# Moving vector work of stages 2 to 4 and of the keys onto GpSimd and ScalarE in an eight-block cross-attention network

## The chip, the cores and the metric

The kernel runs on one core of a Trainium2 chip, as one program of 39,917 instructions. A core has five engines with an instruction queue each: TensorE (PE in the profile, with its weight loads as PEld) multiplies matrices and transposes by multiplying with an identity; VectorE (DVE), ScalarE (ACT) and GpSimd (POOL) work on tiles of 128 partitions; SyncE (SP) starts most DMAs. Engines run their own queues in order and wait for each other through semaphores. The metric is device microseconds (us) from start to end. Before the change the median of 3 runs was 3399.83 us (3399.31 to 3401.43).

## The reference

The input x is four sequences of 512 tokens with 512 features (2,048 tokens). Eight blocks are applied one after the other, alternating cross-attention and feed-forward, each on a layer-normalised x, gated and added:

```python
x = x + jnp.tanh(g_xattn[1]) * _L1_xattn_ref(_layernorm(x), ctx_1024, ...)
x = x + jnp.tanh(g_ffn[1])   * _L1_ffn_ref(_layernorm(x), weight, w_scale, bias)
x = x + jnp.tanh(g_xattn[2]) * _L2_xattn_ref(ctx_1024, _layernorm(x), ...)
```

These three are the kernel's stages 2, 3 and 4, which the change touches. Stage 2 makes attention weights from the context (four sequences of 512 rows with 256 features) and mixes x's features with them:

```python
energy = jnp.einsum('bnd,bmd->bnm', query, key)
attention = jax.nn.softmax(energy, axis=-1)
x_m = jnp.einsum('bln,bmn->blm', teacher_logits, attention)
```

Stage 3 is a quantised linear layer, with one scale per token:

```python
absmax = jnp.max(jnp.abs(x), axis=-1, keepdims=True)
scale = jnp.maximum(absmax, eps) / 127.0
q = jnp.clip(jnp.round(x / scale), -128, 127).astype(jnp.int8)
acc = jnp.einsum('bsk,nk->bsn', q, weight, preferred_element_type=jnp.int32)
out = acc.astype(jnp.float32) * in_scale * w_scale[:, 0] + bias
return out.astype(jnp.float16)
```

Stage 4 is a state-space layer: its scan result y depends on the context alone, and only its last step, `y = y * silu(z)` with z the normalised x, needs the x of that moment. Stage 5 is a mixture of experts that begins with normalisation and a router product. Stage 6, much later, is an attention whose keys and values come from the context alone (`ctx @ Wkv`, 32 heads of 16), with a rotation of the keys by position:

```python
out = jnp.stack([x1 * cos - x2 * sin, x1 * sin + x2 * cos], axis=-1)
```

## The kernel before

All of x stays in SBUF as 16 tiles of 128 tokens by 512 features. A batch b is one sequence, that is four tiles t. The stages run one after the other, each as a loop over four batches (`NB`) with an inner loop over four tiles (`TB`). The class `Net` has small helpers, which appear in the profile under their own lines: `ln` (L193, statistics at L175 and L176, a square root on ACT at L179, the normalising DVE instruction at L200), `lnT` (normalise, transpose on PE at L218, copy out of PSUM through `evict`), `transposed` (four PE transposes at L228 and one copy), `chain` (a chain of matrix products into one PSUM bank, L238) and `residual` (L729, one DVE instruction that does x += r * gate). `evict(i, ...)` copies a PSUM bank to SBUF, on ACT (L161) when i is odd and on DVE (L163) when it is even.

Stage 2 (`s2`, L813), per batch: queries and keys from the context (L238, bias on DVE), then for each tile m the energies (PE, L834), the negated row maximum (DVE, L839), the exponential with its sum (ACT, L841), the reciprocal (DVE, L842), the division by the sum (DVE, L843) and the transposition of the weights into aT; then `lnT` of x, and for each tile a product of four matrix multiplications and the residual.

Stage 3 (`s3`, L856), per batch: normalise four tiles, absolute maxima (DVE, L869), scales. Then for each tile, scale and round to an integer by adding MAGIC = 1.5 * 2^23 (DVE, L877), shift back and clip below (DVE, L880), clip above and convert to bf16 (DVE, L882), four transposes (PE, L886), a copy qT (alternately DVE and ACT), the product po (PE, L238), the dequantisation r (DVE, L892), bias and conversion to float16 (DVE, L896), the residual (DVE, L729).

Stage 4 (`s4`, L1082), per batch: the stored y by DMA, normalise x into g, SiLU over all four tiles in one ACT instruction (L1093, with a load of the function table), four products g * y (DVE, L1095), then for each tile four transposes (PE, L1099) and the residual. Its normalisation needs only its own batch of x, so a batch of stage 4 can begin while stage 3 is at work on the next.

Beside these three stages, a generator `keys()` computes stage 6's keys and values. There are 16 of them, one for each tile of context. Each step makes the product `pkv` (16 matrix multiplications, two banks: keys and values), rotates the keys with six DVE instructions that read PSUM (`rope`, L1426 to L1429, into one of two padded tiles `ropes`), copies the values on ACT (L1514) and stores them, and then transposes and stores the keys of the step before (`keyT`, PE L1447, ACT L1531). The function `aside(n)` draws n such steps into the stage at the place where it is called: two per batch in `s2`, one in `s3`, one in `s4`.

The order on each engine is not written by hand. The framework's scheduler goes over the whole program when it is built, with the place in the program as priority, and fixes the order of every engine's queue; `aside` lifts its instructions a little:

```python
def aside(n):
    with tc.high_priority(offset=-400):
        for _ in range(n):
            next(keys, None)
```

Tiles come from pools of rotating buffers: the pool `tp` gives 512-wide working tiles (tag "t", ten of them), `ps1` single PSUM banks (four), `ps2` double banks (two, shared by pkv and the transposed keys), `wp` 2,048-wide tiles (eight). A new tile waits until the last reader of the buffer's former content is done.

Of the kernel before, what the change touches and what calls it, by code (L numbers as in the profile page):

```python
# [9 lines left out]
F32 = mybir.dt.float32  # L10
# [5 lines left out]
AF = mybir.ActivationFunctionType  # L16
ALU = mybir.AluOpType
AX = mybir.AxisListType

P = 128  # L20
# [4 lines left out]
TB = S // P  # L25
# [23 lines left out]
class Net:  # L49
# [153 lines left out]
            outs.append(xl)  # L203
        return outs

    def lnT(self, name, b, rows=None, room=None):

        nc = self.nc
        xl = self.ln(name, self.x[b * TB : (b + 1) * TB])
        if rows is not None:  # L210
            for i in range(TB):
                t = b * TB + i
                nc.sync.dma_start(rows[t * P : (t + 1) * P, :], xl[i])
        xT = (room or self.u)(f"xT_{name}").rearrange("p (c n) -> p c n", c=DC)
        for c in range(DC):
            pt = self.mm(f"pt_{name}_{c}")
            for i in range(TB):
                nc.tensor.transpose(  # L218
                    pt[:, i * P : (i + 1) * P], xl[i][:, c * P : (c + 1) * P], self.ident
                )  # L220
            self.evict(c, xT[:, c, :], pt)
        return xT

    def transposed(self, name, src, dst, i=0, tied=False):
# [585 lines left out]
    def s2(self, aside):  # L810
# [5 lines left out]
        for b in range(NB):  # L816
# [15 lines left out]
            for m in range(TB):  # L832
                pe = self.mm(f"s2_pe_{b}_{m}")
                nc.tensor.matmul(  # L834
                    pe, lhsT=qk[0][:, m * P : (m + 1) * P], rhs=qk[1], start=True, stop=True
                )
                nmx = self.s(f"s2_nmx_{b}_{m}", 1, "s2_nmx")
                sm = self.s(f"s2_sm_{b}_{m}", 1, "s2_sm")
                nc.vector.tensor_reduce(nmx, pe, axis=AX.X, op=ALU.max, negate=True)  # L839
                at = self.t(f"s2_at_{b}_{m}")  # L840
                nc.scalar.activation(at, pe, AF.Exp, bias=nmx, accum_out=sm)  # L841
                nc.vector.reciprocal(sm, sm)  # L842
                nc.vector.tensor_scalar(at, at, sm, None, op0=ALU.mult)  # L843
                self.transposed(f"s2_{b}_{m}", at, aT[:, :, m * P : (m + 1) * P], m)
            xT = self.lnT(f"s2_{b}", b, room=self.w)
            aside(2)
            for t in range(TB):
                po = self.mm(f"s2_po_{b}_{t}")
# [6 lines left out]
    def s3(self, aside):  # L855
# [5 lines left out]
        nc.vector.tensor_copy(w, w8.bitcast(I8))  # L861
        wsc = self.bcast("s3_wsc", a["s3_wsc"])
        bias = self.bcast("s3_bias", a["s3_bias"])
        for b in range(NB):
            xl = self.ln(f"s3_{b}", self.x[b * TB : (b + 1) * TB])
            aside(1)
# [8 lines left out]
            for t in range(TB):  # L875
                q = xl[t]
                nc.vector.tensor_scalar(  # L877
                    q, q, rsc[:, t : t + 1], MAGIC, op0=ALU.mult, op1=ALU.add
                )
                nc.vector.tensor_scalar(q, q, -MAGIC, -128.0, op0=ALU.add, op1=ALU.max)  # L880
                qb = self.tp.tile([P, 512], BF16, tag="t", name=f"s3_q_{b}_{t}")
                nc.vector.tensor_scalar(qb, q, 127.0, None, op0=ALU.min)  # L882
                pt = self.ps1.tile([P, 512], BF16, tag="mm", name=f"s3_pt_{b}_{t}")
                for c in range(DC):
                    cs = slice(c * P, (c + 1) * P)
                    nc.tensor.transpose(pt[:, cs], qb[:, cs], self.ident16)  # L886
                qT = self.tp.tile([P, 512], BF16, tag="t", name=f"s3_qT_{b}_{t}")
                self.evict(t, qT, pt)
                po = self.mm(f"s3_po_{b}_{t}")
                self.chain(po, [(qT[:, c * P : (c + 1) * P], w[:, c, :]) for c in range(DC)])  # L890
                r = self.t(f"s3_r_{b}_{t}")
                nc.vector.scalar_tensor_tensor(  # L892
                    r, po, isc[:, t : t + 1], wsc, op0=ALU.mult, op1=ALU.mult
                )
                h = self.tp.tile([P, 512], F16, tag="t", name=f"s3_h_{b}_{t}")
                nc.vector.tensor_tensor(h, r, bias, op=ALU.add)  # L896
                self.residual(b * TB + t, h, self.gf[:, 1:2])


# [183 lines left out]
    def s4(self, aside):  # L1083
        nc = self.nc
        EC = DC
        for b in range(NB):
# [5 lines left out]
            self.ln(f"s4_{b}", self.x[b * TB : (b + 1) * TB], out=g)  # L1092
            nc.scalar.activation(g4, g4, AF.Silu)  # L1093
            for e in range(EC):
                nc.vector.tensor_tensor(g[:, e, :], g[:, e, :], y[:, e, :], op=ALU.mult)  # L1095
            for t in range(TB):
                pt = self.mm(f"s4_pt_{b}_{t}")
                for e in range(EC):
# [316 lines left out]
        self.wt5 = wt  # L1415


    def rope(self, name, ps, t, out):

        nc = self.nc  # L1420
        H = 32
        x = ps.rearrange("p (m h k) -> p m h k", m=2, h=H)
        cos, sin = (v[:, t, :].unsqueeze(1).to_broadcast([P, H, 8]) for v in self.trig)
        for i in range(2):
            tmp = self.t(f"rt_{name}_{i}")[:, 0 : H * 8].rearrange("p (h k) -> p h k", h=H)
            dst = out[:, :, 8 * i : 8 * i + 8]  # L1426
            nc.vector.tensor_tensor(tmp, x[:, 1, :, :], (sin, cos)[i], op=ALU.mult)
            nc.vector.tensor_tensor(dst, x[:, 0, :, :], (cos, sin)[i], op=ALU.mult)
            nc.vector.tensor_tensor(dst, dst, tmp, op=(ALU.subtract, ALU.add)[i])  # L1429

    def padded(self, name, n, fill):

# [18 lines left out]
    def keys(self):  # L1451
# [52 lines left out]
        for b in range(NB):  # L1504
            cx = self.context("s6", b)
            for k in range(TB):
                ks = slice(k * P, (k + 1) * P)
                pkv = self.sc(f"s6_pkv_{b}_{k}")
                for i in range(2):
                    half = slice(512 * i, 512 * (i + 1))  # L1510
                    self.chain(pkv[:, i, :], [(cx[:, c, ks], wkv[:, c, half]) for c in range(CC)])
                self.rope(f"k_{b}_{k}", pkv[:, 0, :], b * TB + k, ropes[k % 2])
                v = vs[k % 2]
                nc.scalar.copy(  # L1514
                    v[:, 0 : H * 17].rearrange("p (h d) -> p h d", d=17)[:, :, 0:16],
# [459 lines left out]
```

## Time and profile before

| What | Value |
|---|---|
| Median of 3 runs | 3399.83 us |
| Profiled execution (its span) | 3401.39 us (3399.4 us) |
| PE busy | 2880.1 us, 85% of the span |
| DVE busy | 1975.8 us, 58% |
| ACT busy | 1197.1 us, 35% |
| POOL busy | 627.9 us, 18% |
| Mean granted TensorE clock | 0.920 of full speed |
| Stage 2 | about 1527 to 1678 us |
| Stage 3, and stage 4 beside it | about 1678 to 1811 us |
| End of stage 4, start of stage 5 | about 1811 to 1853 us |

The span is the time from the first instruction to the last in one execution; the time of that execution lies 2.0 us above it. The busy shares are means over the whole program. The three stretches at the bottom are 326 us, about a tenth of it, so the shares say little about them; each has to be read by itself. A line of the tables by group reads: source line, engine, operation, output<-input by the program's names, shape and count, then busy us and mean ns of one, then the time that the engine was idle just ahead of these instructions and what ended it. In the tables of waits, "A <- B" says that A waited for B. The granted clock is the share of full speed at which the chip's throttle let PE run.

### The profile page before, as it was taken

How to read it: one execution, taken by the hardware profiler on the slowest of the kernel's cores; microseconds unless marked ns; L12 is line 12 of the kernel's file. 1: busy time of each engine (PE TensorE's matmuls, PEld its weight loads, DVE VectorE, ACT ScalarE, POOL GpSimd, SP SyncE). 2: the span in 40 equal slices, each digit the busy share in tenths (PEclk: the TensorE clock that was granted, in tenths of full speed). 3: DMA queues.
4: the chain of work that ended last, by engine and by line, in shares of the span. 5: the costliest groups of instructions: out<-in, count | busy, mean ns of one | idle time of the engine just before them, and what ended most of it. 6: DMA issues, size and time to landing. Idle time of an engine off the chain costs nothing.

```text
span 3399.4 us, 39917 instructions
## 1 busy us (share of the span) xinstructions
PE 2880.1 (85%) x14620; PEld 1432.3 (42%) x14624; DVE 1975.8 (58%) x3148; ACT 1197.1 (35%) x1927; POOL 627.9 (18%) x509
## 2 busy tenths in 40 slices
PE   4889898968998989998836699968898988889995
PEld 2333333223444444444414588842233332244673
DVE  5555555558797989975687311137666666634103
ACT  1243333355544454433222111112544444520231
POOL 0000000005564655760000122210000000000341
PEclk9799999988998999999967699987999999989997
DMA  3000000047675876861212599971000000022698
GB/s 125 7 1 7 1 1 9 1 160 227 195 230 177 241 223 202 250 188 57 84 63 85 177 324 325 325 250 50 13 27 13 27 1 1 1 75 78 245 385 314
DMA packets 266338, 438.56 MB, mean 129 GB/s; under 512 B 32368, under 2 KB 114544, under 8 KB 264608
## 3 DMA queue, kind: packets, MB, share of 16 engines
q1 hardware_dynamic: 247776, 382.52, 35.3%
q0 software_dynamic: 13760, 45.10, 3.7%
q10 hardware_dynamic: 4608, 8.39, 0.7%
q8 instruction: 117, 1.92, 0.2%
q14 instruction: 77, 0.63, 0.1%
HBM read 370.79 MB, written 65.13 MB: 128 GB/s over the span
## 4 chain that ended last, share of the span: by engine, by line
PE 38%; DVE 9%; issue 3%; DMA 2%; POOL 2%; ACT 1%; SPq 0%; POOLq 0%; DVEq 0%; ACTq 0%
PE s_po L238 8%; PE s_pl L262 7%; PE pg_s L238 6%; PE s_av L262 4%; DVE s_top L1656 2%; PE s_ph L238 2%; PE s_pq L238 2%; PE s_ps L262 1%; PE s_pkv L238 1%; PE s_pr L238 1%; DVE x L729 1%; DMA s_y<-s_ys 1%; PE pt_s L218 1%; POOL s_ys L1321 1%; PE s_pb L238 1%
## 5 line engine op out<-in xcount | busy, mean ns | idle before, releaser
L1012 POOL TENSOR_TENSOR s_h<-s_h,s_C 128x512 f32<-128x512 f32 x256 | 447.2, 1747 | 295.7 <-DVE s_h L1011 249.7
L1656 DVE TENSOR_REDUCE s_top<-s_ps 128x1 f32<-128x512 f32 x512 | 330.1, 686 | 162.6 <-PE s_ps L262 158.4
L1766 ACT ACTIVATE pr_s<-s_pl 128x512 f32<-128x512 f32 x512 | 277.9, 595 | 344.2 <-PE s_ps L262 327.1
L1011 DVE TENSOR_TENSOR_SCAN s_h<-s_da,s_db 128x512 f32<-128x512 f32 x256 | 312.0, 1219 | 62.8 <-PE s_y L262 37.1
L262 PE MATMUL s_pl<-s_qT,s_kT 32*128 32x512 f32 x1024 | 291.4, 642 | 63.4 <-DVE s_top L1656 59.0
L262 PE MATMUL s_ps<-s_kT,s_qT 32*128 32x512 f32 x1024 | 306.6, 668 | 6.1 <-DVE s_top L1656 5.8
L1010 ACT ACTIVATE s_da<-s_rdl,s_A 128x512 f32<-128x512 f32 x256 | 184.3, 722 | 329.3 <-DVE s_h L1011 328.7
L238 PE MATMUL s_ph<-xT_s,s_wu 128*128 128x256 f32 x1024 | 250.4, 400 | 0.7 <-ACT xT_s L161 0.7
L771 PE MATMUL s_acc<-s_wd,s_hT 128*128 128x512 f32 x512 | 239.9, 612 | 6.8 <-ACT s_hT L802 6.8
L238 PEld LDWEIGHTS s_ph<-xT_s,s_wu 128*128 128x128 f32 x1024 | 199.9, 200 | 79.3 <-issue 48.4
L238 PEld LDWEIGHTS pg_s<-s_xbT,s_w 128*128 128x128 f32 (+1 forms) x1872 | 214.1, 183 | 19.8 <-issue 17.8
L599 DVE TENSOR_REDUCE s_nmx<-ps_s 128x2 f32<-128x992 f32 x128 | 151.4, 1184 | 116.7 <-PE ps_s L262 116.7
L238 PE MATMUL pg_s<-s_xbT,s_w 128*128 128x128 f32 (+1 forms) x1872 | 215.7, 275 | 1.4 <-ACT s_xbT L161 1.4
L262 PE MATMUL s_av<-pr_s,s_v 128*32 128x512 f32 (+1 forms) x1536 | 209.6, 617 | 0.8 <-ACT pr_s L1766 0.7
L1009 DVE TENSOR_TENSOR s_db<-s_B,s_rdu 128x512 f32<-128x512 f32 x256 | 202.7, 792 | 10.5 <-DMA s_B<-s_bc 2.7
L714 ACT ACTIVATE pr_s<-pl_s 128x1024 f32<-128x1024 f32 (+1 forms) x128 | 130.9, 1022 | 192.1 <-PE pl_s L262 161.7
L262 PE MATMUL s_y<-s_h,ident 64*64 64x512 f32 x1024 | 146.5, 635 | 47.1 <-issue 30.0
L1400 DVE TENSOR_TENSOR g_s<-g_s,pg_s 128x256 f32<-128x256 f32 x78 | 27.5, 353 | 263.9 <-ACT g_s L1399 263.9
L262 PEld LDWEIGHTS s_pl<-s_qT,s_kT 32*128 32x128 f32 x1024 | 80.0, 184 | 232.9 <-ACT pr_s L1766 197.7
L262 PE MATMUL pl_s<-s_qT,s_kT 32*128 32x512 f32 (+1 forms) x512 | 151.1, 667 | 26.1 <-ACT pr_s L714 23.0
L262 PE MATMUL ps_s<-s_kT,s_qT 32*128 32x496 f32 x512 | 156.1, 713 | 4.5 <-DVE s_nmx L599 4.1
L771 PEld LDWEIGHTS s_acc<-s_wd,s_hT 128*128 128x128 f32 x512 | 93.4, 192 | 151.9 <-issue 116.4
(376 smaller groups left out, 4269.7 us busy)
## 6 DMA issues: line engine op xcount, KB each, us to landing
s_B<-s_bc SPq DMA_DIRECT2D x256, 256.0 KB
s_C<-s_bc SPq DMA_DIRECT2D x256, 256.0 KB
s_w<-in_s_wg SPq DMA_DIRECT2D x39, 704.0 KB
s_w<-in_s_wu SPq DMA_DIRECT2D x39, 704.0 KB
s_w_rt<-in_s_ru SPq DMA_DIRECT2D x47, 512.0 KB
s_w_rt<-in_s_rd SPq DMA_DIRECT2D x47, 512.0 KB
s_w<-in_s_wd SPq DMA_DIRECT2D x39, 512.0 KB
s_y<-s_ys SPq DMA_DIRECT2D x32, 512.0 KB
```

Source lines behind the costliest of these rows:

```text
L218: nc.tensor.transpose(pt[:, i * P : (i + 1) * P], xl[i][:, c * P : (c + 1) * P], self.ident)
L238: ins = self.nc.tensor.matmul(out, lhsT=l, rhs=r, start=(i == 0), stop=(i == len(pairs) - 1)).ins
L262: ins = self.nc.tensor.matmul(out, lhsT=l, rhs=r, **flags).ins
L599: i = nc.vector.tensor_reduce(nmx[:, at : at + 2], ps[:, :, 0:M], axis=AX.X, op=ALU.max, negate=True,)
L714: nc.scalar.activation(prs[i][0:n], pl[0:n], AF.Exp)
L771: ins = nc.tensor.matmul(accs[i][t], lhsT=hT[:, j, t * P : (t + 1) * P], rhs=wd[f // 4][:, f % 4, :], start=(f == 0), stop=(f == FC - 1),).ins
L1009: nc.vector.tensor_tensor(db, br, du, op=ALU.mult)
L1010: nc.scalar.activation(da, dl, AF.Exp, scale=am[:, e, n : n + 1])
L1011: nc.vector.tensor_tensor_scan(h, da, db, 0.0, op0=ALU.mult, op1=ALU.add)
L1012: nc.gpsimd.tensor_tensor(h, h, cr, op=ALU.mult)
L1656: ins = nc.vector.tensor_reduce(dst[:, i], ps[i], axis=AX.X, op=ALU.max, negate=True).ins
L1766: exps.append(nc.scalar.activation(prs[i][:, j, :], pl[j], AF.Exp).ins)
```

## The change

Work is put on other engines in five places; what is computed stays the same, and so do tiles and loops.

- Stage 2: the division of the weights by their sum goes from DVE to ACT; all copies of transposed weights and of transposed x go to ACT instead of alternating.
- Stage 3: the clip becomes one DVE instruction on the values that still carry MAGIC; the shift back by MAGIC, with the conversion to bf16, becomes an ACT activation with a bias tile `less`; the copy qT is always on ACT; the bias is added on GpSimd; the conversion to float16 is a copy on ACT.
- Stage 4: the products g * y go from DVE to GpSimd.
- Keys: ACT copies the key half of pkv to an SBUF tile `kr` (two buffers), and the six rotation instructions run on GpSimd from there.

```diff
     def lnT(self, name, b, rows=None, room=None, turns=(0, 1)):
...
-            self.evict(c, xT[:, c, :], pt)
+            self.evict(turns[c % 2], xT[:, c, :], pt)
...
                 nc.vector.reciprocal(sm, sm)
-                nc.vector.tensor_scalar(at, at, sm, None, op0=ALU.mult)
-                self.transposed(f"s2_{b}_{m}", at, aT[:, :, m * P : (m + 1) * P], m)
-            xT = self.lnT(f"s2_{b}", b, room=self.w)
+                nc.scalar.mul(at, at, sm)
+                self.transposed(f"s2_{b}_{m}", at, aT[:, :, m * P : (m + 1) * P], 1)
+            xT = self.lnT(f"s2_{b}", b, room=self.w, turns=(1, 1))
...
         bias = self.bcast("s3_bias", a["s3_bias"])
+        less = self.s("s3_less", 1)
+        nc.gpsimd.memset(less, -MAGIC)
...
-                nc.vector.tensor_scalar(q, q, -MAGIC, -128.0, op0=ALU.add, op1=ALU.max)
+                nc.vector.tensor_scalar(
+                    q, q, MAGIC - 128.0, MAGIC + 127.0, op0=ALU.max, op1=ALU.min
+                )
                 qb = self.tp.tile([P, 512], BF16, tag="t", name=f"s3_q_{b}_{t}")
-                nc.vector.tensor_scalar(qb, q, 127.0, None, op0=ALU.min)
+                nc.scalar.activation(qb, q, AF.Identity, bias=less)
...
-                self.evict(t, qT, pt)
+                self.evict(1, qT, pt)
...
+                nc.gpsimd.tensor_tensor(r, r, bias, op=ALU.add)
                 h = self.tp.tile([P, 512], F16, tag="t", name=f"s3_h_{b}_{t}")
-                nc.vector.tensor_tensor(h, r, bias, op=ALU.add)
+                nc.scalar.copy(h, r)
                 self.residual(b * TB + t, h, self.gf[:, 1:2])
...
             for e in range(EC):
-                nc.vector.tensor_tensor(g[:, e, :], g[:, e, :], y[:, e, :], op=ALU.mult)
+                nc.gpsimd.tensor_tensor(g[:, e, :], g[:, e, :], y[:, e, :], op=ALU.mult)
...
-    def rope(self, name, ps, t, out):
-
-        nc = self.nc
+    def rope(self, name, ps, t, out, engine=None):
+
+        engine = engine or self.nc.vector
...
-            nc.vector.tensor_tensor(tmp, x[:, 1, :, :], (sin, cos)[i], op=ALU.mult)
-            nc.vector.tensor_tensor(dst, x[:, 0, :, :], (cos, sin)[i], op=ALU.mult)
-            nc.vector.tensor_tensor(dst, dst, tmp, op=(ALU.subtract, ALU.add)[i])
+            engine.tensor_tensor(tmp, x[:, 1, :, :], (sin, cos)[i], op=ALU.mult)
+            engine.tensor_tensor(dst, x[:, 0, :, :], (cos, sin)[i], op=ALU.mult)
+            engine.tensor_tensor(dst, dst, tmp, op=(ALU.subtract, ALU.add)[i])
...
-                self.rope(f"k_{b}_{k}", pkv[:, 0, :], b * TB + k, ropes[k % 2])
+                kr = self.kp.tile([P, 512], F32, tag="kr", name=f"s6_kr_{b}_{k}", bufs=2)
+                nc.scalar.copy(kr, pkv[:, 0, :])
+                self.rope(f"k_{b}_{k}", kr, b * TB + k, ropes[k % 2], nc.gpsimd)
```

## The prediction

> **What bounds the kernel now.** I read the view of the core first (mean granted clock 0.920), then the page's slices to find stages 2 to 4 (about 1527 to 1855 us), then the table of windows over that stretch, its groups of instructions, its waits and its chain of waits. The table has length, then busy time (and instructions) of PE, weight loads, DVE, ACT and POOL, then the granted clock:
>
> ```profile
> 1527.00:1678.00 151.00, 126.26 (x410) 63.88 (x410) 90.36 (x219) 46.98 (x79) 0.00 (x0) 0.98 0.22 71
> 1678.00:1811.00 133.00, 67.59 (x241) 32.36 (x244) 108.12 (x245) 28.34 (x33) 0.00 (x0) 0.71 0.19 61
> 1811.00:1853.00 42.00, 24.07 (x113) 16.45 (x112) 33.40 (x77) 10.65 (x14) 0.00 (x0) 0.77 0.14 49
> ```
>
> Stage 2 is PE's: 84% busy at almost full clock. In stage 3 DVE is busy 81% and PE half, at a reduced clock. POOL does nothing in any of them. The groups of 1678 to 1853 (busy us and mean ns, then idle before) and the waits of 1526 to 1856 say who waits for whom:
>
> ```profile
> L892 DVE SCALAR_TENSOR_TENSOR s_r<-s_po,s_isc,s_wsc 128x512 f32<-128x512 f32 x16 | 12.0, 751 | 22.5 <-PE s_po L238 22.5
> ...
> L896 DVE TENSOR_TENSOR s_h<-s_r,s_bias 128x512 f16<-128x512 f32 x16 | 11.0, 688 | 0.3
> ...
> L1095 DVE TENSOR_TENSOR s_g<-s_g,s_y 128x512 f32<-128x512 f32 x16 | 10.3, 683 | 0.2 <-ACT s_g L1093 0.2
> ```
>
> In the waits (waiter, releaser, total us, times, longest):
>
> ```profile
> PEld L886 <- DVE s_q L882: 57.5, 12, 17.8
> ```
>
> PE waits 57.5 us for the quantised tile; DVE waits 22.5 us for the product that PE then makes. So stage 3 is no queue of DVE work alone: within a batch it is a ring, and between batches a DVE stretch. The ring in the chain of waits (start, length, step), batch 1, tiles 2 to 3:
>
> ```profile
> 1734.69 0.76 DVE s_r L892
> ...
> 1735.48 0.69 DVE s_h L896
> ...
> 1737.06 0.59 ACT s_qT L161
> ...
> 1737.70 1.08 PE s_po L238 x4
> ...
> 1738.80 0.76 DVE s_r L892
> ```
>
> One turn is 4.1 to 4.5 us: L892, L896, L882 (420 ns in the groups, between s_h and s_qT), four transposes, the copy, the product. From L892's starts in the timeline the three turns take 13.10, 13.27, 16.99 and 16.99 us in batches 0 to 3 (60.35), and the stretches between batches 16.70, 20.71 and 16.72 (54.13). In batches 2 and 3 the product takes 1.89 instead of 1.04 us. In the tail PE's timeline shows keys standing behind stage 4's last batch, and the chain going through the rotation and a key's product (another follows at 1845.61):
>
> ```profile
> 1829.96 3.76 PE L1099 MATMUL s_pt<-ident,s_g 128*128 128x128 f32 x16 [11.56 <-DVE s_g L1095]
> ...
> 1838.92 4.70 PE L238 MATMUL s_pkv<-s_wkv,ctx_s 128*128 128x512 f32 x8 [0.38 <-ACT s_vs L1514]
> ```
>
> **Prices and the Trainium skill.** POOL's only like work is stage 4's scan (min/median/max ns, then two lines of its timeline):
>
> ```profile
> L1012 POOL TENSOR_TENSOR s_h<-s_h,s_C x256: 1264/1772/3506, 779.3 to 1510.7; 128x512 f32<-128x512 f32 x128
> ...
> 1493.23 0.70 DVE L1009 TENSOR_TENSOR s_db<-s_B,s_rdu 128x512 f32<-128x512 f32 x1
> 1493.28 1.77 POOL L1012 TENSOR_TENSOR s_h<-s_h,s_C 128x512 f32<-128x512 f32 x1 [2.48 <-DVE s_h L1011]
> ```
>
> "SBUF — State Buffer", Who interferes with whom, says that DVE and GpSimd exclude each other for a whole instruction when DVE has two SBUF inputs or a two-port mode. The trace agrees: POOL takes 1.26 us at best and 1.77 beside DVE's 0.70 product. "GPSIMD Engine Reference", 3.1, gives about 2.6 cycles an element at 1.2 GHz for two inputs. Half of a 512 row is then 0.55 us less than 1.264: I estimate 0.71 us for a 256-wide rotation step (no run shows one; bounds 0.6 and 1.3, the upper with contention). "ScalarE: Activation LUTs", What ACT_TABLE_LOAD costs, has 280 + 0.833 N ns for an ACTIVATE with a pointer operand, 707 at 512; the exponential here takes 687, so I take 0.7 for the new division and the last shift. Copies are 0.59 (s_qT) in the trace. "TensorE: Matmul & The Clock Gate", What's actually happening, says that an idle PE falls to half clock; the windows agree (1.00 at 1685 to 1705, 0.50 at 1745 to 1765).
>
> **The change, part by part.** The built programs' order shows where each instruction now stands; durations are of the profiled run.
>
> Removed from DVE in stages 3, 4 and the tail: L896 16 x 0.69, L882 16 x 0.42, eight s_qT copies x 0.42, L1095 16 x 0.68, and 51 rotation steps x 0.41: 11.0 + 6.7 + 3.4 + 10.3 + 21 = 52 us of busy time. The new clip replaces L880 at its 0.42. This would be the gain only if DVE's busy time were the length.
>
> Stage 2. The division goes from 0.49 on DVE to 0.7 on ACT: +0.2 on the path for the first tiles of a batch; for tile 3 it had queued behind normalisation, and saves some 0.3. All eight matmul records of a key's product now stand ahead of the next tile's transposes, where half (1.88) lay under the softmax: +0.5 to +1.7 in three batches, taken as 0.6. The xT copies, all on ACT at 0.59, keep up with PE, which uses one block per 0.43 and started after 1.75: nothing, or 1.2 lost without that cover. Sum +2 (-2 to +6). The rotation leaves DVE under PE's 13.7 us of products: nothing.
>
> Start of stage 3. PE goes from stage 2's last product into two keys' products and then s3's transposes, which no longer wait for the rotation's 14 steps on DVE: first L892 3.0 earlier. On POOL its bias stands behind one key's six steps: +1.4. Sum -1.6.
>
> The ring, the part that decides. DVE's order in the changed program is L892, then that tile's residual, which waits for ACT's copy of h, which waits for POOL's bias. On ACT the copy of h of tile t stands ahead of the shift of tile t+1. So a turn is L892 0.75, POOL 1.27, h 0.60, shift 0.70, to the copy 0.55 (transposes, as from L882's end to s_qT now), copy 0.58, product 1.04, and 0.2 of gaps: 5.7 us; 6.6 where the product takes 1.89. What was one DVE queue step of 0.69 plus 0.42 is now four steps on two engines. Batch 0: 3 x 5.7; batch 1: 5.7 + 2 x 6.6; batches 2 and 3: 6 x 6.6: 75.6. POOL also has four gate products (5.1 us) ahead of a bias in batches 2 and 3, started by ACT's SiLU, which itself stands ahead of h: +1.5 and +2.5. Sum 79.6 against 60.35: +19. This assumes that PE stays cold; if it doesn't, 5.7 x 12 + 4 = 72.4, +12.
>
> Between batches. DVE's front (four normalisations 0.46, four maxima 0.6, statistics, scale and clip) reaches the first clipped tile in 9.5 after L892, with the residual's wait in it; ropes and stage 4's normalisation no longer stand in it. POOL's rotation steps contend with it, +1. Then shift 0.7, transposes 0.55 to copy, the second half of a key's product 1.7 in between, product 1 to 1.9: 5. So 15.5 each, and 2.3 more where gate products stand ahead of the last bias of batch 2: 48.8 against 54.13: -5.3.
>
> Tail. From the end of the last L892 (1810.96) to the first router product (1854.65) are 43.7 us. Now: last bias 1.3, a key's four last steps to 4.2, its transposes to 6.3, stage 4's transposes with a key's product among them to 15.8 (K half 12.3), copy and rotation to 17.2, the next key's product to 21, its rotation to 25; table load and SiLU on ACT to 27; four gate products on POOL, behind all rotations, to 32.1; transposes, then four residuals on DVE ahead of the router's first copy: 36.4. Sum -7.3 (-12 to 0). What is late next there is POOL.
>
> Sum: +2 - 1.6 + 19 - 5.3 - 7.3 = +6.8 on a profiled execution of 3401.39 us (span 3399.4). That execution is 1.6 over the median of 3399.83, within the runs' own spread, so I add to the median: 3406.6, forecast 3407. Below 0.2% (6.8 us) I call it no change, as far as a measurement tells.
>
> **Rivals.** (a) Faster, 3390: PE keeps its clock and POOL's rotation hides. For: POOL is idle now, and DVE loses 52 us. Place: the ring, at the turn of 5.7 instead of 6.6 in all batches (-7), with no front contention (-3) and gate products never ahead of a bias (-6.3): -16 to -17. It decides once transposes and product see a clock above about 0.8. Against: PE idles over 60% of a turn. (b) A tie, 3400: the tail gives back 12 rather than 7 and stage 2 is free; 6.8 - 4.7 - 2 = 0. For: PE's 11.56 us wait goes. (c) GpSimd becomes the bound, 3424: steps at 1.3 us instead of 0.71. Some 30 of the 96 steps lie on the path (start, tail, ahead of biases): 30 x 0.59 = 18 more. For: the 1772 median against 1264. Against: DVE often waits while POOL works.
>
> **How the numbers follow.** Forecast's case 0.38 (own range 3400 to 3416), (a) 0.28, (b) 0.17, (c) 0.17. Faster 0.30: (a) and a little of (b). Same 0.22: most of (b) and the forecast's lower edge. Slower 0.48: the rest of the forecast and (c). Range 3383 to 3426: to (c) above, and below (a) by its unknown tail (5 more) and stage 2 (2 more).
>
> **What would show it.** After: L892's starts 5.7 to 6.6 us apart; DVE idle ahead of the residual of h with ACT as releaser, some 2 us each; DVE busy in 1678 to 1811 below 75 us; the 51 steps on POOL near 0.71; the tail near 36 us. Wrong if turns stay under 5 us, if POOL's steps take over 1 us, or if stage 2 grows by over 6 us.

## The result and the profile after

The changed kernel takes 3409.15 us (median of 10 runs, 3402.56 to 3414.07), the kernel before in the same comparison 3399.42 us (10 runs, 3393.55 to 3406.23). The ratio is 1.0027, with a 95% interval of 1.0018 to 1.0036: slower by 9.7 us, where the forecast was 7. The profiled execution of the changed kernel took 3413.88 us, 4.7 us above its median, so two profiles side by side show more (12.5 us) than the medians do.

The change does what it says with the load of the engines. Over the whole program DVE's busy time falls from 1975.8 to 1915.7 us, POOL's rises from 627.9 to 742.7 and ACT's from 1197.1 to 1248.7. The stages' windows of the changed kernel, at its own borders (length, busy time and count of PE, weight loads, DVE, ACT and POOL, granted clock):

```profile
1529.40:1696.60 167.20, 140.39 (x426) 71.96 (x427) 68.94 (x161) 68.37 (x118) 34.47 (x48) 0.90 0.21 64
1696.60:1832.00 135.40, 66.09 (x225) 29.66 (x228) 74.67 (x140) 53.69 (x77) 58.47 (x55) 0.65 0.19 60
1832.00:1864.40 32.40, 24.13 (x126) 18.10 (x125) 28.89 (x58) 14.09 (x18) 21.66 (x25) 0.87 0.34 116
```

In stage 3, DVE is now busy 55% instead of 81%, and the stage is longer: from the end of stage 2's last product to the last dequantisation it takes 134.7 us where it took 125.4. No engine is full (PE 49%, ACT 40%, POOL 43%), so what sets the time is looked for in the waits. Those of 1690 to 1865 name the links of a chain through several queues (waiter, releaser, total us, times, longest):

```profile
PEld L890 <- ACT s_q L886: 49.1, 14, 6.1
ACT s_h L901 <- POOL s_r L899: 47.1, 14, 4.4
POOL s_r L899 <- DVE s_r L896: 42.4, 11, 5.6
...
DVE x L729 <- ACT s_h L901: 25.2, 15, 3.2
```

PE waits for ACT's shift, ACT for GpSimd's bias, GpSimd for DVE. The chain of waits shows one turn of stage 3's ring, batch 1, tiles 1 to 2 (start, length, step); L886 is the new shift, L899 the bias, L901 the conversion:

```profile
1744.94 0.76 DVE s_r L896
...
1745.77 1.27 POOL s_r L899
...
1747.07 0.62 ACT s_h L901
1747.68 0.63 ACT s_q L886
...
1748.36 0.62 PE s_pt L890 x4
...
1749.06 0.59 ACT s_qT L161
...
1749.70 1.90 PE s_po L238 x4
...
1751.63 0.76 DVE s_r L896
```

This is the ring that the prediction described: 6.69 us a turn where it was 4.35, with the shift of one tile directly behind the conversion of the tile before. In the tail, POOL is now the last: the timeline of PE shows the wait for the last rotated key, and that of POOL the four gate products behind all rotations.

```profile
1854.65 1.97 PE L1452 MATMUL pt_s6k<-ident,s_k_r 128*128 128x128 f32 x8 [4.47 <-POOL s_k_r L1434]
```

```profile
1854.58 5.12 POOL L1100 TENSOR_TENSOR s_g<-s_g,s_y 128x512 f32<-128x512 f32 x4
```

In stage 2, PE's timeline of the kernel before shows the first and the last two softmax tiles of batch 0 (L228 transposes a tile's attention weights, L218 transposes x; in brackets PE's idle time ahead):

```profile
1540.73 0.66 PE L228 MATMUL ptr_s<-ident,s_at 128*128 128x128 f32 x4 [1.24 <-DVE s_at L843]
...
1548.48 0.63 PE L228 MATMUL ptr_s<-ident,s_at 128*128 128x128 f32 x4 [2.41 <-DVE s_at L843]
...
1552.70 0.63 PE L228 MATMUL ptr_s<-ident,s_at 128*128 128x128 f32 x4 [2.73 <-DVE s_at L843]
1553.16 1.91 PE L218 MATMUL pt_s<-ident,xl_s 128*128 128x128 f32 x16
```

The same instructions in the changed kernel:

```profile
1541.54 0.66 PE L228 MATMUL ptr_s<-ident,s_at 128*128 128x128 f32 x4 [2.51 <-ACT s_at L843]
...
1549.66 1.12 PE L228 MATMUL ptr_s<-ident,s_at 128*128 128x128 f32 x4 [2.54 <-ACT s_at L843]
...
1555.04 1.12 PE L228 MATMUL ptr_s<-ident,s_at 128*128 128x128 f32 x4 [2.55 <-ACT s_at L843]
1555.95 3.62 PE L218 MATMUL pt_s<-ident,xl_s 128*128 128x128 f32 x16
```

The last two gaps are not longer to speak of (2.54 and 2.55 us, where they were 2.41 and 2.73), but the same work takes almost twice as long. TensorE's clock fell: the window of stage 2 has 0.90 where it had 0.98. Other gaps did grow. The first tile of batch 0 waits 2.51 instead of 1.24 us, and the third tile of the other batches 2.55 to 2.61 instead of 0.60: in the kernel before, four of a key's products filled that wait, and in the changed kernel all eight stand ahead of the transposes of the tile before.

The stretch from the first product of stage 2 to the first router product of stage 5, cut in the same way for every kernel, carries the comparisons below. "Stage 2" runs from that first product to the end of its last one; "turns" are the twelve times from one dequantisation to the next within a batch; "between" the three such times from one batch to the next; "tail" runs from the last dequantisation to the router. The total also has the start of stage 3 (10.9 us before, 9.0 after). Each row is one profiled execution, in us; a difference of a few us between two rows can be one between two executions. (Of the 12.5 us between the two profiles, 10.2 lie in this stretch; the rest lies outside it, where nothing was changed.)

| Kernel | Stage 2 | Turns | Between | Tail | Total |
|---|---|---|---|---|---|
| before | 155.0 | 60.4 | 54.1 | 44.4 | 324.8 |
| after | 167.2 | 83.2 | 42.5 | 33.1 | 335.0 |
| e1_s2 | 157.6 | 57.6 | 54.1 | 44.9 | 323.9 |
| e2_keys | 164.9 | 62.2 | 40.0 | 33.8 | 308.4 |
| e3_s3 | 155.0 | 77.2 | 58.6 | 44.1 | 345.8 |
| e4_gate | 155.0 | 59.9 | 56.3 | 48.1 | 330.2 |
| f1_bias_back | 164.9 | 52.2 | 42.0 | 30.6 | 298.6 |
| f2_keys_late | 160.4 | 62.2 | 41.2 | 33.9 | 305.2 |
| f3_fill | 158.0 | 83.1 | 41.7 | 33.1 | 324.9 |
| f4_late_shift | 159.1 | 51.4 | 40.9 | 31.0 | 291.4 |
| g1_pipe | 165.2 | 53.0 | 52.0 | 36.0 | 315.3 |
| g2_shift_fill | 155.1 | 51.4 | 40.9 | 31.0 | 287.5 |
| g3_before_pipe | 156.6 | 37.8 | 56.6 | 50.2 | 312.2 |
| h1_pool_f16 | 167.2 | 55.8 | 43.2 | 34.9 | 310.1 |

### The profile page after: what moved, and what is told of

Its sections match the earlier page's. It is cut to its first block, busy times and chain, and to the rows that moved or that the text cites. A ratio compares the mean times of both kernels' runs of the same rounds, so it can differ in the third digit from the quotient of the medians.

```text
span 3411.9 us, 40026 instructions
## 1 busy us (share of the span) xinstructions
PE 2891.3 (85%) x14620; PEld 1436.7 (42%) x14624; DVE 1915.7 (56%) x2964; ACT 1248.7 (37%) x2015; POOL 742.7 (22%) x638
## 4 chain that ended last, share of the span: by engine, by line
PE 59%; DVE 16%; POOL 7%; ACT 7%; issue 6%; DMA 4%; SPq 0%; DVEq 0%; POOLq 0%; ACTq 0%
PE s_po L238 10%; PE s_pl L262 7%; PE pg_s L238 6%; PE s_ph L238 4%; PE s_av L262 4%; POOL s_h L1017 4%; PE s_pq L238 4%; PE pl_s L262 4%; PE s_pkv L238 3%; DVE s_h L1016 3%; DVE s_top L1663 2%; PE s_acc L771 2%; ACT pr_s L714 2%; PE s_ps L262 1%; DVE s_db L1014 1%
## 5 line engine op out<-in xcount | busy, mean ns | idle before, releaser
L1299 POOL DMA_INDIRECT s_xb<-s_xs,s_from x86 | 83.2, 968 | 373.0 <-PE ptr_s_xb L228 230.6
```

Source lines behind the costliest of these rows:

```text
L1299: self.nc.gpsimd.indirect_dma_start(out=t, out_offset=None, in_=self.sorted[name][1], in_offset=bass.IndirectOffsetOnAxis(ap=fr[:, j : j + ...
```

## The experiments

### Each part alone

First the four parts of the change, each put alone into the kernel before. Each expectation sets a theory T against a rival R.

**e1_s2**, stage 2's part:

```diff
...
-                nc.vector.tensor_scalar(at, at, sm, None, op0=ALU.mult)
-                self.transposed(f"s2_{b}_{m}", at, aT[:, :, m * P : (m + 1) * P], m)
-            xT = self.lnT(f"s2_{b}", b, room=self.w)
+                nc.scalar.mul(at, at, sm)
+                self.transposed(f"s2_{b}_{m}", at, aT[:, :, m * P : (m + 1) * P], 1)
+            xT = self.lnT(f"s2_{b}", b, room=self.w, turns=(1, 1))
```

> The kernel before with stage 2's part alone (division and all copies of transposed tiles on ACT). Theory T, from the two traces: of stage 2's growth of 12.2 us (first L834 chain to last product, 1529.8-1684.8 before, 1529.4-1696.4 after) most comes from this part: each softmax turn grows from 3.85-3.9 to 4.06 us, the gap ahead of the transposes (L228) from 2.3-2.4 to 2.5-2.7, and TensorE's clock drops to half there. It expects stage 2 to grow by 6 to 12 us and the whole by as much: 3406 to 3411, with L228 and L218 at double length in two batches or more. Rival R: the growth comes from the keys' part (eight products ahead of the next tile's transposes, ACT's copies of the key half in the softmax), so this part alone adds 1 to 2: 3400 to 3402.

Measured: 3395.84 us against 3397.59, ratio 0.9997 (0.9989 to 1.0006). Stage 2 grows by 2.6 us, nearly all of it in batch 0 (41.3 instead of 38.8 us), where L218 takes 3.36 us. Theory T falls: the clock does drop in one batch, but this part costs almost nothing, so R's reading, that the growth belongs to the keys' part, remains.

**e2_keys**, the keys' part:

```diff
...
-                self.rope(f"k_{b}_{k}", pkv[:, 0, :], b * TB + k, ropes[k % 2])
+                kr = self.kp.tile([P, 512], F32, tag="kr", name=f"s6_kr_{b}_{k}", bufs=2)
+                nc.scalar.copy(kr, pkv[:, 0, :])
+                self.rope(f"k_{b}_{k}", kr, b * TB + k, ropes[k % 2], nc.gpsimd)
```

> The kernel before with the keys' part alone (copy on ACT, rotation on GpSimd). Theory T: it takes 24 rotation steps out of the stretches between stage 3's batches and 20 out of the tail, worth about 6 there and 7 in the tail, and costs 1 to 4 in stage 2: -9 to -12, 3388 to 3391; GpSimd's steps at 0.73 us, and DVE's normalisation (L200) slower than 0.54 beside them. Rival R1: the growth of stage 2 belongs to this part: stage 2 +8 to +10, the whole -2 to +2, 3398 to 3402. Rival R2: the rotated keys come late and TensorE waits for them (25 us of such waits after): slower, 3404 or more.

Measured: 3381.85 us, ratio 0.9959 (0.9946 to 0.9972), 14 us faster. Both gains are larger than T had (14.1 us between batches, 10.6 in the tail), and stage 2 loses 9.9, as R1 had it; neither total was right, and R2, that waiting for late keys would make the kernel slower, falls. PE's timeline, tile 3 of batch 1, first in the kernel before and then in e2, has a gap of 4.0 us instead of 2.7:

```profile
1590.77 0.63 PE L228 MATMUL ptr_s<-ident,s_at 128*128 128x128 f32 x4 [2.73 <-DVE s_at L843]
1591.23 3.06 PE L218 MATMUL pt_s<-ident,xl_s 128*128 128x128 f32 x16
```

```profile
1593.47 0.86 PE L228 MATMUL ptr_s<-ident,s_at 128*128 128x128 f32 x4 [4.01 <-DVE s_at L843]
1594.12 3.39 PE L218 MATMUL pt_s<-ident,xl_s 128*128 128x128 f32 x16
```

(L218 is slow in both: in this batch the clock falls in the kernel before, too.) DVE's timeline of the same microseconds in e2, with GpSimd rotating from 1587.7 to 1595.5, says why:

```profile
1591.60 0.86 DVE L200 TENSOR_SCALAR xl_s<-x,mv_s,rs_s 128x512 f32<-128x512 f32 x1
1592.38 0.94 DVE L843 TENSOR_SCALAR s_at<-s_at,s_sm 128x512 f32<-128x512 f32 x1
```

The normalisation takes 0.86 instead of 0.54 us and the division 0.94 instead of 0.49. In the changed kernel the division is on ACT and this gap is 2.9 us in batches 1 to 3; in batches 2 and 3 the clock still falls in it (L228 then takes 1.1 us), in batch 1 it does not.

**e3_s3**, stage 3's part:

```diff
...
-                nc.vector.tensor_scalar(qb, q, 127.0, None, op0=ALU.min)
+                nc.scalar.activation(qb, q, AF.Identity, bias=less)
...
-                nc.vector.tensor_tensor(h, r, bias, op=ALU.add)
+                nc.gpsimd.tensor_tensor(r, r, bias, op=ALU.add)
+                nc.scalar.copy(h, r)
```

> The kernel before with stage 3's part alone (one clip on DVE, shift and conversion on ACT, qT on ACT, bias on GpSimd, conversion to float16 on ACT). Theory T: the ring of a batch becomes longer, its twelve turns from 60.4 to 78-83 us (5.6 to 7 us each), and the stretches between batches get back 3 to 6: +14 to +20, 3413 to 3420. Rival R: DVE, 81% busy in this stage, is relieved of 1.5 us per tile and gives the ring's loss back, since rotations and normalisation fill its gaps: within 4 us of before, 3396 to 3404.

Measured: 3424.04 us, ratio 1.0075 (1.0059 to 1.0090), 25 us slower, more than T had. The turns take 77.2 us, just below T's span, but the stretches between batches don't get anything back and lose 4.5. R falls.

**e4_gate**, stage 4's part:

```diff
-                nc.vector.tensor_tensor(g[:, e, :], g[:, e, :], y[:, e, :], op=ALU.mult)
+                nc.gpsimd.tensor_tensor(g[:, e, :], g[:, e, :], y[:, e, :], op=ALU.mult)
```

> The kernel before with stage 4's part alone (gate products on GpSimd). Theory T: where a gate product stands on the path it takes 1.27 instead of 0.68 us, in the tail 5.1 against 2.7 for the four, but between batches DVE has 2.7 us less ahead of the next front in three of four batches: -2 to -6, 3394 to 3398. Rival R: the tail's loss of 2.4 us stands alone, because DVE's front waits for other things: +1 to +3, 3400 to 3403.

Measured: 3400.90 us, ratio 1.0007 (0.9998 to 1.0016). No gain, T falls: the tail loses 3.7 us and the stretches 2.2. A difference this small isn't told from nothing by the runs, and the profiled execution lies 4.9 us above the median; R fits.

The totals of the table add up: -1.0 - 16.4 + 21.0 + 5.4 = +9.0 us, against +10.2 for all four at once (by the ratios of the runs +13 against +9, with intervals that together are wider than that difference). The loss is stage 3's part, and the keys' part pays for three quarters of it.

### What in stage 3's part costs, and where stage 2's time goes

**f1_bias_back** is the changed kernel with the bias as before:

```diff
-                nc.gpsimd.tensor_tensor(r, r, bias, op=ALU.add)
-                nc.scalar.copy(h, r)
+                nc.vector.tensor_tensor(h, r, bias, op=ALU.add)
```

> The changed kernel with bias and conversion to float16 back on DVE as one instruction. Theory T: the ring is long because of the two steps on GpSimd and ACT (1.27 + 0.62 against 0.69 on one queue); it falls from 5.6-8.3 to 4.7-5.7 us a turn, the twelve turns from 83 to 60-66 us, and the whole by 17 to 23: 3386 to 3392. Rival R: the shift on ACT and the colder TensorE hold the ring at 75 or more: 3400 to 3405.

Measured: 3371.24 us, ratio to before 0.9919 (0.9899 to 0.9939), so some 37 us below the changed kernel, more than T had. The turns are 52.2 us, below those of the kernel before. A likely reason is that with the shift on ACT, PE no longer waits for a DVE queue that has the bias of the tile before in it; f4 and g3 below bear on that.

**f2_keys_late** is e2 with keys 0 to 5 left on DVE:

```diff
-                kr = self.kp.tile([P, 512], F32, tag="kr", name=f"s6_kr_{b}_{k}", bufs=2)
-                nc.scalar.copy(kr, pkv[:, 0, :])
-                self.rope(f"k_{b}_{k}", kr, b * TB + k, ropes[k % 2], nc.gpsimd)
+                kr, engine = pkv[:, 0, :], nc.vector
+                if b * TB + k >= 6:
+                    kr = self.kp.tile([P, 512], F32, tag="kr", name=f"s6_kr_{b}_{k}", bufs=2)
+                    nc.scalar.copy(kr, pkv[:, 0, :])
+                    engine = nc.gpsimd
+                self.rope(f"k_{b}_{k}", kr, b * TB + k, ropes[k % 2], engine)
```

> The kernel before with the keys' part for the keys 6 to 15 alone; keys 0 to 5, which are rotated while stage 2 runs, stay on DVE from PSUM. Theory T: stage 2's 9.9 us of growth under the keys' part come from GpSimd's steps beside DVE's division and normalisation there (L200 and L843 at 0.9 instead of 0.5, the gap ahead of tile 3's transposes 4.0 instead of 2.7 us), so stage 2 is back at 155 us and the gains of the later stages stay: -24 to -27 against before, 3371 to 3374. Rival R: stage 2 grows by ACT's copies or by the order of the products, or the later gains hang on the earlier keys: -15 to -17, 3381 to 3383, as with all keys on GpSimd.

Measured: 3376.79 us, ratio 0.9940 (0.9924 to 0.9955). It lies between the two: stage 2 is at 160.4 us, not 155. Batch 1 is at 38.1 us (40.7 in e2, and 39.8 in the kernel before with its slow L218), and its last two gaps are 0.60 and 2.72 again, so the loss that came with the rotation on GpSimd is gone there; batch 3, in which a key still rotates on GpSimd, has 40.9. Batch 0 has 41.6, with L218 at 3.41 us: the clock fell, although the keys of this batch are rotated on DVE. Its later gaps are those of the kernel before (2.31, 2.40 and 2.72 us), but the first is 2.14 instead of 1.24. A case with no such difference is g3, below.

**f3_fill** keeps PE busy in the gaps of the changed kernel's stage 2, with PE's other instructions tied to their order there:

```diff
...
         pt = self.mm(f"ptr_{name}")
+        for _ in range(fill):
+            self.tie(self.nc.tensor.transpose(pt[:, 0:P], self.ident, self.ident).ins)
...
-                self.transposed(f"s2_{b}_{m}", at, aT[:, :, m * P : (m + 1) * P], 1)
+                self.transposed(f"s2_{b}_{m}", at, aT[:, :, m * P : (m + 1) * P], 1,
+                                tied=True, fill=12 if m > 1 or b == 0 else 0)
```

> The changed kernel with twelve transposes of the identity written into the bank of the next transposition ahead of stage 2's weights' transposes (all tiles of batch 0, tiles 2 and 3 of the others), overwritten afterwards; TensorE's order else as in the changed kernel. Theory T: some 8 of stage 2's 12.2 us are the clock, which falls when TensorE waits 2.5 to 2.9 us two or three times in a row. With the gaps filled L228, L218 and L834 stay at full speed and stage 2 takes 157 to 161 instead of 167.2 us: the whole 3399 to 3403. Rival R: the clock's loss is small or the filler brings as much work as it saves: stage 2 at 165 to 169, the whole 3407 to 3412.

Measured: 3397.73 us, ratio to before 1.0005 (0.9996 to 1.0014), against 1.0027 without the filler. PE's timeline in batch 0:

```profile
1549.77 1.47 PE L230 MATMUL ptr_s<-ident 128*128 128x128 f32 x12
1552.48 0.66 PE L232 MATMUL ptr_s<-ident,s_at 128*128 128x128 f32 x4 [1.24 <-ACT s_at L847]
1552.97 1.91 PE L218 MATMUL pt_s<-ident,xl_s 128*128 128x128 f32 x16
```

Useless work (L230) makes the useful work behind it run at full speed: L218 takes 1.91 instead of 3.62 us. Stage 2 falls from 167.2 to 158.0 us and its clock is 0.99; the turns, stretches and tail stay within a microsecond of the changed kernel's. So the clock cost the changed kernel 9.2 us in stage 2. The kernel before lost some 1.7 to it as well, in batch 1 (39.8 us; g3 has the same gaps there, keeps the clock and takes 38.1). Of the growth of 12.2 us, an estimate from these figures is 7.5 for the clock and 4.7 for longer steps.

**f4_late_shift** adds to f2 the shift and all qT copies on ACT, with bias and conversion left on DVE:

```diff
...
-                nc.vector.tensor_scalar(q, q, -MAGIC, -128.0, op0=ALU.add, op1=ALU.max)
+                nc.vector.tensor_scalar(
+                    q, q, MAGIC - 128.0, MAGIC + 127.0, op0=ALU.max, op1=ALU.min
+                )
...
-                nc.vector.tensor_scalar(qb, q, 127.0, None, op0=ALU.min)
+                nc.scalar.activation(qb, q, AF.Identity, bias=less)
...
-                self.evict(t, qT, pt)
+                self.evict(1, qT, pt)
```

> The kernel of f2 (keys 6 to 15 on GpSimd) with stage 3's clip, the shift with conversion on ACT and all qT copies on ACT; bias and conversion to float16 stay on DVE. Theory T: a turn of the ring exchanges 0.42 on DVE for 0.63 to 0.70 and a hand-over on ACT, so the twelve turns lose 3 to 6 us, while DVE is spared 0.42 us for each tile between batches: +0 to +5 against f2. Rival R: DVE's relief decides: -3 to -6 against f2, and this is the best version.

Measured: 3365.20 us, ratio 0.9906 (0.9889 to 0.9923). T falls and R holds, with more than it claimed: the turns go from 62.2 to 51.4 us, although the shift takes 0.72 us on ACT where it took 0.42 on DVE. A step can become slower and its ring shorter, if it leaves a queue in which it stood behind something late. (The qT copies left DVE in the same edit; what each of the two moves is worth was not measured apart.)

### Order or length

**g1_pipe** is the changed kernel with stage 3's loop written one tile ahead:

```diff
-            for t in range(TB):
+            def product(t):
...
+                return po
+
+            following = product(0)
+            for t in range(TB):
+                po = following
+                if t + 1 < TB:
+                    following = product(t + 1)
                 r = self.t(f"s3_r_{b}_{t}")
```

> The changed kernel with stage 3's inner loop written one tile ahead: shift, transposes, copy and product of tile t+1 stand ahead of bias, conversion and residual of tile t, so that ACT's queue no longer has the conversion of tile t ahead of the shift of tile t+1. All operations stay on the engines of the change. Theory T: the ring is a matter of the queue's order, not of the length of the two added steps: a turn falls from 5.6-8.3 to 3.4-4.5 us, the twelve turns from 83 to 42-52, the whole by 28 to 38: 3371 to 3381. Rival R: the steps on GpSimd and ACT are too long in themselves, since the residual behind them holds DVE's queue: turns of 5 us or more, twelve of them 60 or more, 3390 to 3400.

Measured: 3394.29 us, ratio 0.9995 (0.9984 to 1.0006), 11 us below the changed kernel by the ratios (20 between the two profiled executions). That is well short of T's 28 to 38, and the total lies in R's span. The turns do fall, to 53.0 us, just above T's span, but the stretches between rise from 42.5 to 52.0. In the first two (2.0 and 1.8 us longer) the loop's order puts two residuals instead of one behind the last dequantisation of a batch; in the third (5.6 us longer) the chain of waits runs through four gate products on GpSimd (5.73 us from 1776.70) ahead of the rotation of the key that PE takes next. It speaks for T, but not cleanly.

**h1_pool_f16** is the cleaner test. GpSimd keeps the bias and writes float16 itself, so ACT's copy is gone:

```diff
-                nc.gpsimd.tensor_tensor(r, r, bias, op=ALU.add)
                 h = self.tp.tile([P, 512], F16, tag="t", name=f"s3_h_{b}_{t}")
-                nc.scalar.copy(h, r)
+                nc.gpsimd.tensor_tensor(h, r, bias, op=ALU.add)
```

> The changed kernel with the conversion to float16 done by GpSimd in the same instruction as the bias, so that the copy of h leaves ACT's queue; all else as in the change, and the loop is not written ahead. Theory T: what made the ring was ACT's copy of h standing ahead of the next tile's shift, not GpSimd's 1.27 us. With the copy gone the shift of tile t+1 follows qT of tile t at once; a turn is bounded by DVE waiting for GpSimd ahead of the residual (0.75 + 1.27 + 0.75 and hand-overs, 3 us) or by the product at low clock: 3 to 4.5 us, the twelve turns from 83 to 40-52 us; between batches and in the tail nothing is given back as in g1, since the loop's order is that of the change: 22 to 36 below the changed kernel, 3372 to 3386. Rival R: GpSimd's bias is too slow or contends with DVE, turns stay at 5 us or more, twelve of them 60 or more, or the stretches between grow as in g1 (42.5 to 52): 3390 to 3400.

Measured: 3383.76 us, ratio 0.9963 (0.9948 to 0.9977), 22 us below the changed kernel by the ratios. Stage 2 is the same to 0.01 us, the stretches stay at 43.2, and the turns fall from 83.2 to 55.8 us, somewhat above T's span. ACT's timeline shows what left:

```profile
1733.18 0.58 ACT L161 COPY s_qT<-s_pt 128x512 bf16<-128x512 bf16 x1 [0.54 <-PE s_pt L890]
1733.66 0.72 ACT L886 ACTIVATE s_q<-xl_s,s_less 128x512 bf16<-128x512 f32 x1
1735.18 0.58 ACT L161 COPY s_qT<-s_pt 128x512 bf16<-128x512 bf16 x1 [0.79 <-PE s_pt L890]
```

The shift (L886) follows the copy of the tile before at once. In the changed kernel a conversion stood between them, and with it a wait for GpSimd of up to 4.4 us. GpSimd's bias takes the same 1.27 us in both rings. The conversion's own 0.62 us, twelve times, would be 7.4 us; the turns fall by 27.4. Part of that is TensorE's clock: the chain of waits has the product of these tiles at 1.04 us, where the changed kernel's ring has 1.90.

**g3_before_pipe** does to the kernel before what g1 does to the changed one:

```diff
-            for t in range(TB):
+            def product(t):
...
+            following = product(0)
+            for t in range(TB):
+                po = following
+                if t + 1 < TB:
+                    following = product(t + 1)
```

> The kernel before with stage 3's inner loop written one tile ahead as in g1, all operations on their former engines. Theory T: the ring of the kernel before is the same matter of order (conversion L882 of tile t+1 stands behind dequantisation and bias of tile t in DVE's queue), so its turns fall from 4.1-6 to 2.8-3.8 us, the twelve from 60 to 36-45, the whole by 12 to 22: 3375 to 3385. Rival R: DVE's own work and the keys' products between keep the turns as they are: -4 to +2, 3393 to 3399.

Measured: 3386.61 us, ratio 0.9971 (0.9961 to 0.9981), 10 us faster, a little less than T had, without moving one instruction to another engine. The turns fall from 60.4 to 37.8 us; the tail loses 5.8 and the stretches 2.5. The kernel before had the same kind of ring, in DVE's queue. In batch 0 of stage 2, which the edit doesn't touch, PE runs the same instructions in the same order as in the kernel before, with gaps of 1.23, 2.31, 2.40 and 2.73 us (1.24, 2.32, 2.41 and 2.73 there), and L218 still takes 3.02 us instead of 1.91:

```profile
1553.53 3.02 PE L218 MATMUL pt_s<-ident,xl_s 128*128 128x128 f32 x16
```

So the clock can fall with no change to the stage at all.

**g2_shift_fill** is f4 with f3's filler in stage 2.

```diff
...
-                self.transposed(f"s2_{b}_{m}", at, aT[:, :, m * P : (m + 1) * P], m)
+                self.transposed(f"s2_{b}_{m}", at, aT[:, :, m * P : (m + 1) * P], m,
+                                tied=True, fill=12 if m > 1 or b == 0 else 0)
```

> The kernel of f4 (keys 6 to 15 on GpSimd, shift and qT on ACT) with the filling transposes of f3 in stage 2. Theory T: stage 2 falls from 159 to 152-155 us, because part of its time in f4 is still a clock at half: -4 to -7 against f4, 3358 to 3361. Rival R: in f4 the gaps are covered well enough, or the filler delays the transposes: -1 to +3 against f4.

Measured: 3360.57 us, ratio 0.9897 (0.9881 to 0.9914), within T's span. Stage 2 is back at 155.1 us. It is the fastest version that was run, 35 us below the kernel before; its interval overlaps that of f4, so the filler's share in it rests on the profile.

## Why the prediction held, and where it did not

The forecast of 3407 was met within 2.2 us, but four of its five terms were off by more than that: stage 2 and the ring cost 10.2 and 3.8 us more, the stretches between batches and the tail 6.3 and 4.1 less, and these nearly cancelled. That the ring would lose more than the later stages give back was foreseen; that the sum came so close is luck. By its own steps, in the profiled executions:

| Step | Predicted | Measured |
|---|---|---|
| Stage 2 | +2 | +12.2 |
| Start of stage 3 | -1.6 | -1.9 |
| Ring | +19 | +22.8 |
| Between batches | -5.3 | -11.6 |
| Tail | -7.3 | -11.4 |
| Sum | +6.8 | +10.2 |

- **The ring** was right in place and in its chain of waits, and 3.8 us short in size. Turns of 5.6 to 7.0 us in batches 0 and 1 were forecast at 5.7 and 6.6; the shift is measured at 0.72 (0.7 taken), the bias at 1.27 and the conversion at 0.62 (0.60 taken), and DVE waits 1.7 us ahead of each residual, with ACT as releaser (some 2 forecast). The prediction named the link that matters: "On ACT the copy of h of tile t stands ahead of the shift of tile t+1." g1 and h1 show it to be the cause. Its summary, "four steps on two engines", is not: h1 keeps GpSimd's step and f4 a slower shift, and both have short turns.
- **Gate products ahead of biases** were to cost 4 us. Batches 2 and 3 do take 44.7 us, where six undisturbed turns of 6.8 would be 40.8, but hardly for that reason: a bias behind gate products starts at most 0.3 us after its dequantisation ends (at 1818.61 after 1818.34). What the timelines show instead is stage 4's SiLU on ACT ahead of two conversions, as the prediction also said (1789.14 to 1791.05, with the conversion at 1790.96), and what it left out: a square root with its table load ahead of a copy qT (1783.02 to 1784.62) and stage 4's normalisation on DVE ahead of a dequantisation (until 1787.9). That the size came out right is in part luck.
- **Stage 2** was outside the bound that the prediction set for itself (wrong if it grows by over 6). The step that failed is "Sum +2": it priced steps, and these cost some 4.7 us, inside its -2 to +6, but it priced no clock. f3 shows that TensorE's lower clock cost 9.2 us there, about 7.5 more than in the kernel before. The prediction knew of the falling clock and used it in stage 3 only, where PE was already half idle and the clock at 0.71; stage 2, at 0.98, was the place that had a clock to lose.
- **"The rotation leaves DVE under PE's 13.7 us of products: nothing"** was wrong for the same stage: e2 shows the rotation on GpSimd reaching into the softmax of the next batch and slowing DVE's division there.
- **Between batches** the term of 5 us from the first clipped tile to the next dequantisation was too large. In batch 1 to 2 the shift begins at 1768.99 and L896 at 1772.43: 3.4 us. The 2.3 us for gate products ahead of batch 2's last bias did not come either (14.2 us, as in the other stretches). e2 shows the gain to come with the rotation's departure from DVE's queue (14.1 us); the gate adds nothing (e4).
- **The tail** was right in its last link, POOL's four gate products (5.12 us, 5.1 taken), and too long before them: 32.3 us from the end of the last L896 where 36.4 were worked out. PE had a clock of 0.87 there, not 0.77, with its transposes packed between the keys' products.
- **GpSimd's rotation step** was estimated at 0.71 us; the four lines of it have medians of 0.73 to 0.76, and the 48 steps of 1690 to 1865, some of them beside DVE's work, a mean of 0.82. Rival (c), with 1.3, is out.
- **DVE busy below 75 us in stage 3**: 74.7 in the stage's own 135.4 us.

## What to carry to other kernels

Before an operation moves to a less busy engine, look at what it will stand behind in that engine's queue and what will stand behind it: an instruction that waits for a late result holds up the ready one behind it, and that decided more here than either's length. On the kernel before, a loop written one tile ahead was worth 10 us with no instruction moved. And a stage in which PE waits for some 60% of each turn (2.4 of 3.9 us here) can be close to an edge of its clock: the clock fell in one batch of the kernel before and in three of the changed one, where the waits are longer. Filling the waits, which brought the three batches from 44.4, 41.1 and 42.9 us to 40.4, 39.3 and 39.4, gave the loss back.

## What the runs showed of the hardware that was not expected

GpSimd slows DVE, and selectively. Two groups of the kernel before, from 1678 to 1853 (busy us and mean ns of one, then idle before):

```profile
L729 DVE SCALAR_TENSOR_TENSOR x<-s_h,gf,x 128x512 f32<-128x512 f16 x16 | 11.9, 746 | 0.0
...
L200 DVE TENSOR_SCALAR xl_s<-x,mv_s,rs_s 128x512 f32<-128x512 f32 x20 | 9.8, 541 | 0.0
```

The same groups of the changed kernel from 1690 to 1865, and the dequantisation:

```profile
L200 DVE TENSOR_SCALAR xl_s<-x,mv_s,rs_s 128x512 f32<-128x512 f32 x17 | 14.9, 919 | 0.0
L729 DVE SCALAR_TENSOR_TENSOR x<-s_h,gf,x 128x512 f32<-128x512 f16 x16 | 14.0, 877 | 25.2 <-ACT s_h L901 25.2
...
L896 DVE SCALAR_TENSOR_TENSOR s_r<-s_po,s_isc,s_wsc 128x512 f32<-128x512 f32 x16 | 12.0, 750 | 34.8 <-PE s_po L238 34.6 <-PE s_pkv L238 0.2
```

L200 takes 919 ns where it took 541, the residual L729 877 where it took 746. Within the changed kernel, L729 takes 0.75 us while GpSimd is idle (at 1708.37) and 1.35 beside its gate products (at 1791.59). L896, one of whose two wide inputs is in PSUM, stays at 750 (751 before), beside gate products too (at 1795.57 and 1817.59). This agrees with "SBUF — State Buffer", Who interferes with whom, in the Trainium skill, which has DVE instructions with two SBUF inputs, and tensor_scalar in its two-port mode, share an interface with GpSimd; that L200 runs in that mode is not shown here. The prediction quoted that place for POOL's price and charged each stretch 1 us; L200 alone lost 17 x 0.38 = 6.4 us of DVE's time over those 175 us.

TensorE's clock fell in short gaps. In batch 0 of the changed kernel three of 2.51 to 2.55 us, with 1.5 us of work between, were enough, and in batch 1 of the kernel before it fell behind gaps of which none was longer than 2.73. "TensorE: Matmul & The Clock Gate", What's actually happening, in the Trainium skill names a whole idle window of about 3.4 us as the condition; no gap in these two cases was that long, so here the measurement decides. How little activity lets the clock fall was not measured. The same section says that the window runs freely and that one kernel varies by it, and that agrees: batch 0 of stage 2 took 38.8 us in the kernel before and 40.5 in g3, which has the same instructions there in the same order.
